# Roots of the norms by logarithm and exponential on ScalarE, merged key and query products, and the first norms on VectorE

## The chip, the cores and the metric

The kernel runs on one core of a Trainium2 chip. The metric is the device time in microseconds of one execution. A core has TensorE (PE; its weight loads are listed as PEld), VectorE (DVE), ScalarE (ACT), GpSimd (POOL) and SyncE (SP), which work through their own queues in order and wait for one another by semaphores; DMA queues move data beside them.

## The reference

A sequence of 8 x 512 tokens with 128 features, x of shape (8, 512, 128) in float32, goes through four residual layers, each on a normalised copy of x:

```python
x = x + _L0_attn_ref(_layernorm(x), ...)   # a gated linear scan over time
x = x + _L0_ffn_ref(_layernorm(x), ...)    # one 128x128 matrix, picked by argmax
x = x + _L1_attn_ref(_layernorm(x), ...)   # delta rule over time, 16 heads of 8
x = x + _L1_ffn_ref(_layernorm(x), ...)    # 8 experts, the best 2 for each token
```

`_layernorm` is `(x - mean) / sqrt(var + 1e-5)`. The first layer divides its two matrices W_in and W_out by their largest singular values, if these are over 1. Its scan has coefficients that are normalised per element. The third layer normalises a second time inside, makes query, key, value and a gate beta for every token, divides the key by its norm over the 8 features of a head, and runs, for every head,

```python
retrieval = S @ k_t
S = S + outer(beta_t * (v_t - retrieval), k_t)
o_t = S @ q_t
```

over the 512 steps. The fourth layer routes every token to two experts with 512 hidden units, gelu between the two products.

## The kernel before

**Tiling.** Tokens are taken in 32 tiles of 16 time steps x 8 sequences = 128 rows. Four tiles make a group (`g` from 0 to 7). For every group there is a first part (`first_layers`: `scanned`, `ssm_out`, `linear`), a preparation of the delta rule (`delta_in`), the delta rule itself (`delta_rule`), and routing (`route`). One or two groups together then go through the experts (`experts`): their rows are scattered by destination to DRAM with indirect DMAs of GpSimd, taken in blocks of 128 rows of one expert each, and gathered back.

**The delta rule.** It is sequential in time. A tile is done in four blocks of four steps, and inside a block the four steps are solved at once with a small triangular matrix (`tm`, the T matrix, the trace's `tmat`), which is made from the products of keys of a block at distance one, two and three and from beta. For each of the 128 blocks VectorE runs six instructions, each needing the one before: a product `so` of keys and queries with the state, a sum over it, the product with the T matrix (`prod`), a sum, the product with keys, and a sum that is the new state. Keys and queries in the layout for this come from `scratch` in DRAM into `kq`. Products of queries with keys inside a block go into `planes` (`qkp`) and then to the output matmuls.

**Norms.** `moments` takes sums of four tiles with VectorE's `bn_stats`. `factors` makes from them the factor 1/sqrt(var + eps) and the shift -mean times that factor, on GpSimd: a multiply-add (two if the second normalisation inside the delta layer is made at once, `norms == 2`), a power -0.5 against the constant `mhalf`, a product with the mean and a multiplication by -1. `normalised` applies factor and shift tile by tile on ScalarE. There are four norms for each group: of the input (`i`), after the first layer (`a`), before the delta rule (`b`, with both factors), and before the experts (`e`). The trace has them as `small_mvi`, `small_rstdi`, `small_shifti`, and with a, b and e.

**Products at a distance.** In `delta_in` six GpSimd instructions write `pd` (key with key one step apart, and three apart), `pc` (key with key and query with key, two apart) and `pb` (query with key, one and three apart); a seventh writes `pa` (the same step). TensorE then sums them over a head with `head_ones`.

**Singular values.** `spectral` squares each of the two matrices 24 times, with a division by the trace each third time; every squaring is a matmul, then a copy or scaling out of PSUM: VectorE's for the first matrix, ScalarE's for the second. `gain` comes from both.

**The order.** Instructions are not issued as they are written: a recorder (`Recorder`, `Plan`) keeps them with a number each, and `ORDER`, a list of all numbers, says in which sequence they go to the engines. Each engine takes its own in that sequence. A load of ScalarE's function table is put wherever the next function needs another set than the one loaded: logarithm and exponential are in one set (`LN_EXP`), tanh and gelu in another (`GELU_TANH`).

Of the kernel before, what the change touches and what calls it, by code (L numbers as in the profile page):

```python
# [9 lines left out]
F32 = mybir.dt.float32  # L10
# [3 lines left out]
ALU = mybir.AluOpType  # L14
# [344 lines left out]
def _cost(engine, name, n, kw):  # L359
# [28 lines left out]
    1, 7, 53, 56, 105, 50, 0, 13, 418, 54, 58, 115, 4, 17, 47, 55, 63, 41, 5, 6, 61, 9, 18, 40, 2, 3, 57, 8, 15, 60,  # L388
    422, 11, 14, 48, 74, 59, 16, 19, 108, 32, 10, 20, 45, 12, 23, 49, 46, 109, 44, 22, 338, 43, 67, 69, 110, 21, 354,
    70, 71, 111, 24, 30, 42, 324, 112, 25, 330, 26, 346, 113, 114, 27, 116, 124, 325, 126, 117, 72, 118, 339, 125,  # L390
    123, 326, 127, 327, 119, 131, 132, 128, 28, 129, 134, 130, 120, 328, 75, 121, 329, 122, 135, 65, 133, 388, 77,
    331, 138, 73, 386, 136, 139, 873, 347, 148, 137, 51, 387, 147, 66, 362, 390, 141, 355, 140, 341, 149, 153, 107,
    389, 142, 146, 391, 33, 150, 392, 83, 151, 85, 29, 154, 143, 84, 156, 454, 82, 393, 152, 37, 144, 145, 106, 88,
    157, 155, 35, 394, 89, 340, 158, 370, 322, 160, 80, 39, 76, 395, 31, 159, 161, 332, 170, 34, 163, 169, 333, 36,
    86, 171, 90, 162, 378, 175, 164, 334, 172, 78, 396, 62, 91, 178, 38, 165, 397, 68, 168, 173, 174, 166, 176, 167,
    335, 348, 179, 398, 177, 182, 336, 92, 180, 403, 399, 356, 181, 357, 183, 184, 402, 349, 192, 185, 191, 190, 401,
    193, 186, 342, 198, 194, 197, 358, 423, 195, 337, 400, 187, 359, 188, 189, 81, 405, 196, 200, 199, 52, 406, 93,
    202, 350, 201, 404, 407, 203, 204, 206, 205, 87, 207, 212, 351, 214, 213, 408, 208, 220, 215, 352, 209, 219, 210,
    343, 211, 409, 221, 222, 216, 217, 410, 224, 218, 223, 225, 94, 411, 95, 226, 229, 228, 96, 97, 227, 371, 230,
    98, 234, 236, 363, 235, 102, 231, 237, 99, 242, 104, 232, 241, 233, 412, 238, 100, 244, 239, 240, 243, 101, 245,  # L400
    246, 413, 248, 247, 249, 250, 258, 414, 251, 257, 456, 259, 256, 252, 263, 260, 264, 103, 455, 261, 262, 266,
    253, 458, 254, 459, 255, 267, 460, 265, 353, 415, 344, 270, 268, 457, 271, 269, 416, 461, 462, 272, 273, 279,
    417, 278, 274, 285, 286, 280, 420, 275, 276, 463, 288, 277, 281, 287, 282, 290, 419, 283, 464, 284, 424, 289,
    291, 421, 292, 425, 294, 293, 79, 379, 296, 295, 427, 297, 298, 465, 466, 299, 302, 303, 426, 307, 300, 345, 304,
    308, 301, 311, 309, 312, 428, 305, 429, 306, 310, 313, 430, 431, 314, 315, 316, 467, 317, 468, 318, 319, 320,
    360, 321, 469, 323, 471, 432, 474, 433, 472, 491, 592, 434, 373, 470, 364, 435, 436, 380, 473, 372, 365, 437,
    438, 475, 381, 439, 476, 440, 443, 441, 444, 442, 448, 445, 477, 446, 382, 447, 361, 490, 478, 449, 450, 479,
    451, 452, 480, 453, 522, 523, 525, 524, 481, 526, 593, 482, 527, 528, 529, 483, 530, 539, 531, 540, 532, 533,
    541, 64, 595, 542, 366, 594, 374, 367, 543, 536, 383, 544, 484, 375, 485, 545, 546, 486, 547, 537, 488, 596, 548,
    487, 549, 492, 554, 550, 376, 534, 552, 493, 551, 555, 553, 597, 563, 598, 599, 600, 556, 558, 560, 564, 601,  # L410
    561, 565, 557, 569, 559, 566, 660, 489, 570, 571, 574, 662, 575, 494, 602, 495, 576, 572, 661, 578, 573, 704,
    577, 603, 562, 579, 496, 497, 580, 498, 581, 499, 628, 567, 582, 500, 587, 568, 583, 1212, 502, 516, 606, 703,
    584, 588, 501, 585, 503, 663, 589, 608, 504, 586, 664, 368, 505, 590, 665, 506, 666, 510, 667, 668, 509, 669,
    508, 591, 670, 702, 607, 604, 671, 672, 535, 673, 629, 674, 605, 538, 675, 507, 676, 612, 610, 511, 677, 512,
    513, 678, 514, 679, 609, 680, 515, 681, 613, 377, 682, 517, 746, 689, 683, 690, 614, 744, 684, 691, 611, 685,
    518, 692, 686, 693, 745, 694, 705, 687, 695, 615, 519, 688, 706, 520, 696, 616, 707, 708, 617, 709, 697, 710,
    698, 618, 699, 711, 700, 521, 1143, 1142, 1213, 712, 1144, 619, 713, 1145, 384, 714, 1146, 715, 1214, 716, 620,
    717, 1147, 385, 718, 1148, 719, 621, 1152, 720, 721, 1149, 722, 1150, 1153, 1159, 723, 622, 1160, 724, 1151, 731,
    788, 725, 623, 732, 726, 1161, 1162, 786, 727, 733, 1215, 734, 728, 735, 787, 729, 736, 747, 1163, 737, 730, 748,
    624, 1164, 749, 1157, 750, 626, 751, 738, 752, 739, 1166, 740, 753, 741, 625, 1165, 742, 754, 1154, 755, 1167,  # L420
    627, 756, 743, 630, 1168, 757, 1172, 758, 1169, 759, 1170, 1174, 760, 1173, 1171, 761, 762, 1175, 763, 1178,
    1180, 764, 1176, 1183, 1181, 765, 1217, 1216, 1218, 1219, 1177, 1185, 701, 773, 766, 1194, 774, 1184, 767, 775,
    776, 768, 1179, 1220, 1182, 769, 1282, 777, 1280, 778, 770, 1189, 771, 789, 1221, 1281, 1186, 1156, 790, 779,
    1226, 772, 1190, 791, 792, 793, 780, 1191, 794, 1195, 1228, 631, 1227, 1196, 1192, 1198, 1222, 1193, 795, 1232,
    796, 1197, 781, 1233, 782, 828, 783, 1223, 633, 784, 797, 798, 799, 800, 632, 1199, 634, 801, 635, 1155, 636,
    1200, 637, 802, 1224, 803, 1201, 804, 805, 1234, 806, 785, 638, 1202, 1235, 807, 1203, 808, 1225, 1204, 815,
    1324, 640, 816, 1561, 1236, 1205, 817, 639, 818, 819, 809, 820, 641, 810, 642, 821, 811, 822, 812, 1207, 813,
    1323, 643, 1283, 1206, 1284, 814, 1208, 1285, 1322, 1286, 1237, 1287, 644, 1229, 1288, 823, 645, 824, 1289, 825,
    646, 649, 1230, 648, 826, 1290, 650, 647, 1291, 1292, 827, 1187, 651, 652, 829, 1231, 1293, 1188, 1294, 653,
    1238, 1295, 1209, 1296, 1297, 655, 1298, 1211, 1299, 1210, 654, 1300, 1239, 1249, 1301, 830, 1302, 831, 1240,  # L430
    656, 1366, 1303, 657, 658, 1304, 832, 1309, 1563, 1305, 833, 1310, 1241, 659, 1564, 1311, 1365, 1312, 1307, 1313,
    1492, 834, 1314, 1315, 1306, 1308, 835, 838, 1491, 837, 1316, 839, 1325, 836, 1493, 1494, 1562, 1317, 1326, 1495,
    1318, 1242, 1327, 1566, 1328, 1567, 1243, 840, 1329, 841, 1319, 1330, 1565, 1496, 1568, 1502, 1320, 1331, 1497,
# [209 lines left out]
def seq_kernel(  # L643
# [384 lines left out]
    def factors(mv, part, norms=1, bufs=2):  # L1028
# [4 lines left out]
        if norms == 2:  # L1033

            nc.gpsimd.tensor_scalar(rstd[:, 1], mv[:, :, 2], (1.0 + LN_EPS) / P, LN_EPS * LN_EPS, ALU.mult, ALU.add)
# [845 lines left out]
```

## Time and profile before

| what | value |
|---|---|
| median of 3 runs | 692.75 us (692.0 to 696.13) |
| the profiled execution | 694.65 us, span 693.0 us |
| granted TensorE clock, mean | 0.867 |
| busy: PE, VectorE, ScalarE, GpSimd | 514.9, 483.1, 465.4, 546.3 us |
| first and last `so` of the delta rule start at | 101.0 and 565.8 us |
| loads of ScalarE's table by the order's changes of set | 44 |

Times in the profile are microseconds from the start of the span. A group's line gives line, engine, operation, what it writes and reads, shapes and count, then busy time and the mean of one in ns, then the idle time of the engine ahead of it with what ended it. A line of waits gives who waited for whom, the total, how often, and the longest. A stage's line gives busy time and number of instructions of PE, PEld, VectorE, ScalarE, GpSimd, then the clock, the DMA share and GB/s. Nearly all instructions have the recorder's line L335, so they are told apart by the tiles they write.

### The profile page before, as it was taken

To read this page: it belongs to the slowest core of one execution; us is meant where nothing else is said; L and a number is where in the kernel's file an instruction comes from. 1 tells how busy PE (TensorE), PEld (TensorE's weight loads), DVE (VectorE), ACT (ScalarE), POOL (GpSimd) and SP (SyncE) were. 2 spreads that over 40 slices of the span, in tenths; PEclk is the share of its full clock that TensorE was granted. 3 is DMA by queue.
4 is the path that set the end of the run, shared out by engine and by line. 5 is a ranking of instruction groups with operands and counts; after the bars stand their busy time and mean duration, and the time that the engine had idled before them with its cause. 6 is when DMAs were issued, how large, how long until landed. Compare 5 with 4: busy or idle time off the path is not lost. (4 is left out here: it accounts for less than half of the span.)

```text
span 693.0 us, 10892 instructions
## 1 busy us (share of the span) xinstructions
PE 514.9 (74%) x2948; PEld 399.2 (58%) x2948; DVE 483.1 (70%) x1276; ACT 465.4 (67%) x1087; POOL 546.3 (79%) x682
## 2 busy tenths in 40 slices
PE   4886576876769777963768878877889769979970
PEld 3663224544348445652636766666668758978860
DVE  4565169999997899995899999878999970300111
ACT  2876757768775697883785988843986445846640
POOL 5566776699899979998869999987898886786634
PEclk9976586789788987997988999997999898999995
DMA  4991062352184636445346765555799855789852
GB/s 116 288 282 43 0 168 61 101 116 73 37 225 129 170 93 151 109 122 157 113 124 155 180 166 145 161 155 146 190 238 257 217 159 159 219 233 261 252 161 76
DMA packets 94977, 107.48 MB, mean 155 GB/s; under 512 B 8667, under 2 KB 68006, under 8 KB 94918
## 3 DMA queue, kind: packets, MB, share of 16 engines
q1 hardware_dynamic: 89616, 97.97, 52.1%
q0 software_dynamic: 4160, 8.53, 4.6%
q8 instruction: 25, 0.41, 0.3%
q10 hardware_dynamic: 1142, 0.29, 0.2%
q14 instruction: 34, 0.28, 0.1%
HBM read 84.93 MB, written 27.61 MB: 162 GB/s over the span
## 5 line engine op out<-in xcount | busy, mean ns | idle before, releaser
L335 ACT ACTIVATE hid<-ph,w1b 128x128 f32<-128x128 f32 x396 | 117.4, 376 | 53.6 <-PE ph L335 31.3
L335 PE MATMUL ph<-xbT,w1b 128*128 128x128 f32 x792 | 127.9, 292 | 13.3 <-DMA w1b<-w1b_dram 8.0
L335 PEld LDWEIGHTS ph<-xbT,w1b 128*128 128x128 f32 x792 | 112.1, 205 | 25.0 <-issue 11.2
L1595 PE MATMUL po<-w_sb,hid 128*128 x704 | 114.4, 288 | 5.2 <-DVE small_place L335 1.4
L1595 PEld LDWEIGHTS po<-w_sb,hid 128*128 128x128 f32 x704 | 99.1, 201 | 15.7 <-issue 7.5
L335 DVE TENSOR_TENSOR so<-kq,st 128x512 f32<-128x512 f32 x128 | 87.9, 687 | 13.1 <-POOL small_mine L335 7.8
L335 POOL DMA_INDIRECT back<-results,small_dest x64 | 61.9, 968 | 32.9 <-DMA results<-yb 16.2
L1533 POOL DMA_INDIRECT places<-xne,small_dest x64 | 63.6, 993 | 17.9 <-issue 13.5
L335 PEld LDWEIGHTS po<-wo,so 128*128 128x128 f32 x264 | 45.5, 239 | 36.4 <-issue 17.7
L335 DVE TENSOR_REDUCE st<-so 128x32 f32<-128x320 f32 x128 | 63.1, 493 | 4.8
L335 DVE TENSOR_REDUCE st<-st 128x64 f32<-128x320 f32 x128 | 63.6, 497 | 4.0
L335 PE MATMUL po<-wo,so 128*128 128x128 f32 x264 | 51.8, 333 | 19.1 <-DVE x L335 7.9
L335 PE MATMUL in<-b,head_ones 128*128 128x512 f32 x80 | 48.8, 695 | 14.4 <-POOL b L335 6.2
L335 DVE TENSOR_TENSOR st<-kq,st 128x256 f32<-128x256 f32 x128 | 54.6, 426 | 3.9
L304 ACT ACT_TABLE_LOAD x44 | 56.5, 1283 | 0.8
L335 PE MATMUL in<-f,wT 128*128 128x512 f32 x64 | 41.8, 750 | 10.8 <-DVE x L335 4.4
L335 PE MATMUL in<-b,wqkvb 128*128 128x512 f32 x64 | 40.6, 729 | 10.8 <-ACT b L335 3.8
L335 POOL TENSOR_TENSOR qkp<-qkp,upd 128x512 f32<-128x512 f32 x32 | 37.8, 1182 | 10.0 <-ACT upd L335 9.8
L335 DVE SCALAR_TENSOR_TENSOR fin<-back,small_weight,fin 128x128 f32<-128x128 f32 x16 | 5.1, 349 | 57.4 <-DMA back<-results,small_dest 50.1
L335 DVE TENSOR_TENSOR prod<-tmat,st 128x128 f32<-128x128 f32 x128 | 36.5, 285 | 10.3 <-POOL tmat L335 6.9
L335 DVE TENSOR_REDUCE st<-prod 128x32 f32<-128x128 f32 x128 | 37.5, 293 | 7.4 <-ACT upd L335 2.3
L335 POOL TENSOR_TENSOR so<-so 128x512 f32<-128x512 f32 x24 | 30.7, 1280 | 12.1 <-DVE so L335 10.7
(290 smaller groups left out, 1267.6 us busy)
## 6 DMA issues: line engine op xcount, KB each, us to landing
kq<-scratch SPq DMA_DIRECT2D x64, 512.0 KB
w1b<-w1b_dram SPq DMA_DIRECT2D x99, 258.0 KB
xb<-places SPq DMA_DIRECT2D x21, 256.0 KB
results<-yb SPq DMA_DIRECT2D x21, 256.0 KB
places<-yb SPq DMA_DIRECT2D x2, 1472.0 KB
w1b_dram<-in_L_ffn_w_dram SPq DMA_DIRECT2D x1, 2048.0 KB
scratch<-qn SPq DMA_DIRECT2D x8, 256.0 KB
scratch<-kn SPq DMA_DIRECT2D x8, 256.0 KB
```

Source lines behind the costliest of these rows:

```text
L304: self.hw.scalar.preload_act_table_set(switch)
L335: return method(*(on(x) for x in args), **{k: on(x) for k, x in kw.items()})
L1533: rows_out = hw.gpsimd.indirect_dma_start(out=table[0 : nblk * P, :], out_offset=bass.IndirectOffsetOnAxis(ap=at, axis=0), in_=src, in_off ...
L1595: return hw.tensor.matmul(out_.on(nc.banks), lhsT=src, rhs=w2_f[:, bass.ds(at + c * P, P)], start=(c == 0), stop=(c == NHB - 1),)
```

## The change

The power, its constant and the two multiply-adds of `factors` go; ScalarE takes the logarithm of the variance plus eps and the exponential of -0.5 times that, and VectorE makes the shift in one instruction. For group 0 (`leads`) `normalised` runs on VectorE. Key and query of a group lie in one tile (`knq`), and the products with a key one step apart, three apart and two apart are each made for key and query by one GpSimd instruction. The second matrix of `spectral` is copied and scaled by VectorE. The recorded instructions go from 4905 to 4850 (one fewer in each of 32 calls of `factors`, three fewer in each of 8 groups, one constant less, two more), and `ORDER` is a new list.

```diff
 ORDER = (
...
 )
...
-    WIDE = {"both": 2 * N, "xne": P, "w1b": NHB * P + NHB, "drive": N + B, "z": N + B, "kq": NR * QN, "prod": B * BL * BL}
+    WIDE = {"both": 2 * N, "xne": P, "w1b": NHB * P + NHB, "drive": N + B, "z": N + B, "kq": NR * QN, "knq": 2 * N, "dots": 2 * N, "prod": B * BL * BL}
...
-    mhalf = ctile([P, 2, NT], "mhalf")
-    nc.vector.memset(mhalf, -0.5)
...
+        ("eps_col", LN_EPS),
+        ("eps2_col", LN_EPS * LN_EPS),
...
-        nc.gpsimd.tensor_scalar(rstd[:, 0], mv[:, :, 2], 1.0 / P, LN_EPS, ALU.mult, ALU.add)
+        shift = stile([P, norms, NT], "shift" + part, F32, bufs)[:, :, 0:n]
+        spread = mv[:, :, 2]
+        nc.scalar.activation(rstd[:, 0], spread, AF.Ln, bias=eps_col, scale=1.0 / P)
         if norms == 2:
-
-            nc.gpsimd.tensor_scalar(rstd[:, 1], mv[:, :, 2], (1.0 + LN_EPS) / P, LN_EPS * LN_EPS, ALU.mult, ALU.add)
-        nc.gpsimd.tensor_tensor(rstd, rstd, mhalf[:, 0:norms, 0:n], ALU.pow)
-        shift = stile([P, norms, NT], "shift" + part, F32, bufs)[:, :, 0:n]
-        nc.gpsimd.tensor_mul(shift, mv[:, :, 1].unsqueeze(1).to_broadcast([P, norms, n]), rstd)
-        nc.gpsimd.tensor_scalar_mul(shift, shift, -1.0)
+            nc.scalar.activation(rstd[:, 1], spread, AF.Ln, bias=eps2_col, scale=(1.0 + LN_EPS) / P)
+        nc.scalar.activation(rstd, rstd, AF.Exp, scale=-0.5)
+        mean = mv[:, :, 1].unsqueeze(1).to_broadcast([P, norms, n])
+        nc.vector.scalar_tensor_tensor(shift, mean, -1.0, rstd, ALU.mult, ALU.mult)
         return rstd, shift
...
-    def normalised(src, rstd, shift, xn, norm=0):
+    def normalised(src, rstd, shift, xn, norm=0, leads=False):
         for i in range(src.shape[1]):
+            if leads:
+                nc.vector.tensor_scalar(
+                    xn[i], src[:, i, :], rstd[:, norm, i : i + 1], shift[:, norm, i : i + 1], ALU.mult, ALU.add
+                )
+                continue
...
-        nc.scalar.copy(xT, transposed(normalised(x, rstd, shift, tiles_of(xn.rearrange("p (i d) -> p i d", d=D)))))
+        nc.scalar.copy(xT, transposed(normalised(x, rstd, shift, tiles_of(xn.rearrange("p (i d) -> p i d", d=D)), leads=g == 0)))
...
-        nc.scalar.copy(xT, transposed(normalised(x1, rstd, shift, tiles_of(ptile([P, n, D], "f", FIRST)))))
+        nc.scalar.copy(xT, transposed(normalised(x1, rstd, shift, tiles_of(ptile([P, n, D], "f", FIRST)), leads=leads)))
...
-        xh = normalised(x2, rstd, shift, tiles_of(ptile([P, NT, D], "b3")), 1)
+        xh = normalised(x2, rstd, shift, tiles_of(ptile([P, NT, D], "b3")), 1, g == 0)
...
-        normalised(x2, rstd, shift, tiles_of(base))
+        normalised(x2, rstd, shift, tiles_of(base), 0, g == 0)
...
-        kn = ptile([P, N], "kn")
+        kq = ptile([P, 2, N], "knq")
+        kn, qn = kq[:, 0], kq[:, 1]
...
-        qn = ptile([P, N], "qn")
...
-        kb, qb, bb = by_block(kn), by_block(qn), by_block(beta)
-        pa, pb, pc, pd = (ptile([P, N], t) for t in ("b3", "b4", "b2", "b5"))
+        pairs = kq.rearrange("p x (k t) -> p x k t", t=BL)
+        kb, bb = pairs[:, 0], by_block(beta)
+        pa, pc = ptile([P, N], "b3"), by_block(ptile([P, N], "b2"))
+        dots = ptile([P, 2, N], "dots")
+        pd, pb = by_block(dots[:, 0]), by_block(dots[:, 1])
+        both = lambda v: v.unsqueeze(1).to_broadcast([P, 2] + list(v.shape[1:]))
+        apart = dots.rearrange("p x (k t) -> p x k t", t=BL)
         nc.gpsimd.tensor_mul(pa, qn, kn)
-        pb, pc, pd = by_block(pb), by_block(pc), by_block(pd)
-        nc.gpsimd.tensor_mul(pd[:, :, 0:3], kb[:, :, 1:4], kb[:, :, 0:3])
-        nc.gpsimd.tensor_mul(pd[:, :, 3:4], kb[:, :, 3:4], kb[:, :, 0:1])
-        nc.gpsimd.tensor_mul(pc[:, :, 2:4], kb[:, :, 2:4], kb[:, :, 0:2])
-        nc.gpsimd.tensor_mul(pc[:, :, 0:2], qb[:, :, 2:4], kb[:, :, 0:2])
-        nc.gpsimd.tensor_mul(pb[:, :, 0:3], qb[:, :, 1:4], kb[:, :, 0:3])
-        nc.gpsimd.tensor_mul(pb[:, :, 3:4], qb[:, :, 3:4], kb[:, :, 0:1])
+        nc.gpsimd.tensor_mul(apart[:, :, :, 0:3], pairs[:, :, :, 1:4], both(kb[:, :, 0:3]))
+        nc.gpsimd.tensor_mul(apart[:, :, :, 3:4], pairs[:, :, :, 3:4], both(kb[:, :, 0:1]))
+        nc.gpsimd.tensor_mul(
+            pc.rearrange("p k (x t) -> p x k t", x=2), pairs[:, :, :, 2:4], both(kb[:, :, 0:2])
+        )
...
-        nc.scalar.copy(a2, ps[:, :, 2:4])
-        nc.scalar.copy(by_block(planes[:, 1, :])[:, :, 2:4], ps[:, :, 0:2])
+        nc.scalar.copy(a2, ps[:, :, 0:2])
+        nc.scalar.copy(by_block(planes[:, 1, :])[:, :, 2:4], ps[:, :, 2:4])
...
-        spectral(0, nc.vector.tensor_copy, vector_scaled), spectral(1, nc.scalar.copy, nc.scalar.mul)
+        spectral(0, nc.vector.tensor_copy, vector_scaled), spectral(1, nc.vector.tensor_copy, vector_scaled)
...
-        x2 = linear(ssm_out(x, r))
+        x2 = linear(ssm_out(x, r), g == 0)
```

## The prediction

> **What bounds the kernel now.** I read the engine totals first, then the run in three stages (until the first distance product of the delta rule, from there to its last one, and the rest), then VectorE's waits in the middle stage, then the timeline of the first norms.
>
> ```profile
> PE 514.9 (74%) x2948; PEld 399.2 (58%) x2948; DVE 483.1 (70%) x1276; ACT 465.4 (67%) x1087; POOL 546.3 (79%) x682
> ```
>
> The stages (length, then busy time of PE, weight loads, VectorE, ScalarE, GpSimd):
>
> ```profile
> 0.00:101.00 101.00, 67.62 (x230) 41.24 (x231) 50.11 (x174) 64.73 (x149) 66.07 (x100) 0.79 0.54 149
> 101.00:566.50 465.50, 354.83 (x1988) 270.29 (x1986) 414.77 (x1034) 338.53 (x743) 401.57 (x503) 0.88 0.56 148
> 566.50:693.00 126.50, 92.42 (x731) 87.70 (x731) 18.17 (x70) 62.08 (x196) 78.62 (x81) 0.89 0.65 187
> ```
>
> GpSimd is busiest over the whole, but no stage is simply its own. In the first, no engine reaches 68%: a chain of dependent steps sets the time. In the second VectorE holds the chain of 128 blocks (`so` to `st`), and what keeps it waiting is this (engine, what it waited for, us in total, times, longest):
>
> ```profile
> DVE so L335 <- POOL small_mine L335: 7.8, 1, 7.8
> DVE prod L335 <- POOL tmat L335: 6.9, 4, 3.6
> DVE st L335 <- ACT upd L335: 2.3, 3, 1.6
> DVE small_runf L335 <- PE po L335: 2.2, 1, 2.2
> DVE x L335 <- ACT hid L335: 2.2, 1, 2.2
> ```
>
> All waits of that list come to 24.0 us; 15 of them name GpSimd. Without any wait the stage would last 465.5 - 24.0 = 441.5 us, so GpSimd's relief can give no more than that there. The third stage is TensorE's (92.4 of 126.5 us), with the last gather at its end.
>
> The norms of the first stage (start, duration, engine, what). GpSimd makes factors from the moments, then ScalarE applies them:
>
> ```profile
> 62.48 0.20 POOL L335 TENSOR_SCALAR small_rstda<-small_mva 128x4 f32<-128x4 f32 x1
> 62.77 1.02 POOL L335 TENSOR_TENSOR small_rstda<-small_rstda,mhalf 128x4 f32<-128x4 f32 x1
> 63.87 0.20 POOL L335 TENSOR_TENSOR small_shifta<-small_mva,small_rstda 128x4 f32<-128x4 f32 x1
> 64.15 0.23 POOL L335 TENSOR_SCALAR small_shifta<-small_shifta 128x4 f32<-128x4 f32 x1
> ```
>
> ```profile
> 65.30 1.64 ACT L335 ACTIVATE f<-x,small_shifta,small_rstda 128x128 f32<-128x128 f32 x4
> ```
>
> Nothing overlaps this for group 0, since all that follows needs it.
>
> **What the skill says.** "ScalarE: Activation LUTs", section "What ACT_TABLE_LOAD costs": a load takes 1283 ns for every set; the trace agrees:
>
> ```profile
> L304 ACT ACT_TABLE_LOAD x44 | 56.5, 1283 | 0.8
> ```
>
> Its section "Table sets: the hidden batching unit" puts ln and exp in one set and gelu in another, so a pair ln, exp costs one load at most, and one more to come back to gelu. "SBUF — State Buffer", section "Who interferes with whom": a VectorE instruction with two SBUF inputs and a GpSimd instruction that reads SBUF lock each other out. The trace agrees: the subtraction of 128x8 values `sc<-sc,ex` took 1.82 us, ending as GpSimd's 2.35 us sum ended. So less GpSimd work also shortens some VectorE work; I give that no number.
>
> **The change part by part.**
>
> *Factors.* 32 calls (8 groups, four norms). Mean GpSimd times per call: input 0.20+1.03+0.20+0.23 = 1.65; a 0.20+1.05+0.20+0.23 = 1.68; b 2x0.19+1.67+0.21+0.24 = 2.51; e 0.20+1.04+0.32+0.34 = 1.90 us. Times 8: 61.8 us leave GpSimd, some 41 of them in the middle stage (6 a, 7 b, 7 e there by the new order). ScalarE gets 2 instructions per call (3 for b) at 0.20 us: the 128x8 exponentials here took 0.19 to 0.21, a 128x32 one 0.22, so nothing hides in that bound. VectorE gets one of 0.20 us (between 0.14 for a 128x1 and 0.29 for a 128x8 operation).
>
> *Table loads.* Following the two order lists through and counting each change of set: 44 before, as in the trace, and 56 after: by stage 6, 36, 2 and 5, 47, 4. Middle stage of ScalarE: 11 x 1.28 = 14.1, plus 6 x 0.4 + 7 x 0.6 + 7 x 0.4 = 9.4, from 338.5 to 362 us: 79% of a stage of 456 us. Not the bound, if nobody waits for it in order.
>
> *The new wait.* The shift product sits in VectorE's queue and waits for ScalarE's exponential; 20 of them stand between blocks of the delta rule, where earlier VectorE made the moments and went on. In most, 2 to 12 us of other VectorE work stand between moments and shift; in three, under 1.8 us. Behind it wait the next block, then copies and output products. Charge: 20 x 0.23 = 4.6 us of work, and 4 us of waiting (lower end 0, upper end in the third rival).
>
> *Products of a distance.* Six GpSimd products of a group took 0.83+0.43+0.61+0.84+1.15+0.69 = 4.55 us. Three remain, of 768, 256 and 512 elements. These rows run at 2.15 to 3 ns an element:
>
> ```profile
> L335 POOL TENSOR_TENSOR b<-qn,kn 128x384 f32<-128x384 f32 x8 | 9.2, 1146 | 0.0
> L335 POOL TENSOR_TENSOR b<-kn 128x384 f32<-128x384 f32 x8 | 6.6, 827 | 0.3
> ```
>
> So 3.4 to 4.7 us; I take 3.9: 0.65 us a group, 5 us of GpSimd in all. But the first result, which the T matrix needs, comes after 1.9+0.73 instead of 0.83+0.43 us, and now needs the query too: +1.4 us on group 0's path.
>
> *First norms on VectorE, and the second matrix's copies.* 16 normalisations (0.48 us on ScalarE) and 26 copies or scalings (7.7 us in the order's sum) move to VectorE at about 0.29 us (the 128x128 copies there): 12 us more on VectorE in a stage where it idles 51 us; that idle time hides it.
>
> *Path of the first stage.* (1) Until `x1` at 60.0 us: both the 24 squarings and the first scan have to be done. The scan's ScalarE part runs from 21 to 48 us and shares ScalarE with the second matrix; about 16 of its operations there are 5 us. TensorE, in order, waits for those copies too. I take 4 us off (1 to 7). (2) Norm a: moments end at 61.54, factors 64.38, normalised at 66.94: 5.4 us; after: three instructions of 0.2, three hops of 0.06 and 4 x 0.29 = 2.0: -3.4. (3) Norm b: 71.86 to 76.46, 4.6 us; after 2.2: -2.4. (4) Products +1.4. (5) By the order two T matrix steps (1.13+0.37 us) come after the first `so`: -1.5. Sum -9.9: the first `so` at 91 us. The loads of `kq`, issued from 91.1 us on, come 8 us earlier with the key and the query; SP's queue has nothing new ahead of them.
>
> *Middle stage.* 441.5 + 4.6 + 0.8 (two T steps in, one 0.68 us sum out) = 446.9. Remaining waits: of the 24 us, 15 name GpSimd, and another 6 (`x`, `small_runf`, one `upd`) come, followed back, from a GpSimd step late in its queue. GpSimd's work falls from 401.6 by about 46, some 11%. I leave 6 of these waits and add the 4: 456.9, 8.6 less.
>
> *Last stage.* The new list leaves TensorE 164 and 168 expert products where there were 163 and 165; two more loads on ScalarE (2.6 us), mostly beside TensorE's queue; one factor call shorter by 1 us: +1.
>
> Sum: -9.9 - 8.6 + 1 = -17.5. The profiled execution took 694.65 us (span 693.0); it gives 677. The median shown, 692.75, gives **675 us**.
>
> **The rivals.**
> (A) Forecast, 675. For it: almost all of VectorE's waits end in GpSimd, which loses a ninth of its work, and the first norms stand bare on the path.
> (B) The wait moves: GpSimd's bursts stay (64 scatters of 0.99 us in rows of up to 16), so `so` and `tmat` wait as long, 21 us again, plus 4 at the shifts; the middle stage stays at 441.5+5.4+25 = 472, +6; the first gives 10, the last takes 1: 690. A version with half of that gives 683.
> (C) Slower: ScalarE becomes the bound through the in-order shift waits. All else as forecast without its 4 us of waiting gives 21.5; 20 shifts eat that from 1.1 us each on. If a load (1.28) and a gelu row behind it (4 x 0.38 less overlap, about 1.2) stand ahead of each, 2.5 us, it is 50 - 21.5 = 28 slower: 721; at half the shifts 696. Against: by the order most shifts have more VectorE work before them.
> (D) Everything goes: no waits left (446.9) and the first path shorter by 13: -13 - 18.6 + 1: 662.
>
> **Numbers.** Chances: A (668 to 682) 0.50, B (683 to 692) 0.20, C (693 to 721) 0.14, D (656 to 667) 0.16. A measurement tells about 1% (7 us) from no change. Faster by over 1% (below 685.8): A, D and half of B, 0.76. Within 1%: the other half of B and C's mild end, 0.15. Slower: 0.09. The range 660 to 693 leaves out C and the lowest third of D, 0.19 together.
>
> **What would show it.** The first `so` near 91 us; the stage from there to the last near 457; GpSimd about 66 us less busy; 56 loads; `prod<-POOL tmat` and `so<-POOL` waits below 10 us together; shift products with under 5 us of wait. Wrong if VectorE's wait list is led by ScalarE's `small_rstd`, or the first `so` stays near 100.

## The result, and the profile after

| what | before | after |
|---|---|---|
| median of 15 runs | 694.57 us (690.39 to 699.78) | 689.6 us (684.52 to 691.87) |
| ratio, 95% interval | | 0.9917 (0.9887 to 0.9946) |
| profiled execution, its span | 694.65, 693.0 us | 689.16, 687.4 us |
| granted TensorE clock, mean | 0.867 | 0.868 |
| `x` of group 0 after the first layer (x1) | 60.0 us | 65.3 us |
| first and last `so` | 101.0, 565.8 us | 99.5, 561.6 us |

The change gains 5 us, where 17.5 were forecast. Ratios here are always to the kernel before, run beside on the same chip; on three chips, those of e1 to e4, e13 to e16, and e17 and e18, it took 720 us instead of 694, and what these can and can't tell is said with their runs.

The engine totals and one group of the profile after:

```profile
PE 513.5 (75%) x2948; PEld 402.5 (59%) x2948; DVE 504.4 (73%) x1351; ACT 480.3 (70%) x1129; POOL 484.3 (70%) x522
...
L304 ACT ACT_TABLE_LOAD x56 | 71.8, 1283 | 1.0
```

GpSimd lost 62.0 us of work, ScalarE has 12 table loads more: the change does what it says. VectorE has 21.3 us more. The three stages of the kernel after, cut at the same events as before (columns as there):

```profile
0.00:99.50 99.50, 66.44 (x228) 44.07 (x228) 68.02 (x225) 57.05 (x131) 50.39 (x60) 0.79 0.54 150
99.50:562.30 462.80, 356.19 (x1982) 272.94 (x1983) 417.23 (x1054) 357.98 (x797) 360.18 (x387) 0.87 0.55 147
562.30:687.40 125.10, 90.88 (x741) 85.53 (x739) 19.16 (x75) 65.30 (x202) 73.75 (x76) 0.91 0.68 197
```

Against 101.0, 465.5 and 126.5 us, the stages are 1.5, 2.7 and 1.4 us shorter; -9.9, -8.6 and +1 had been forecast. VectorE's waits in the middle stage, after:

```profile
DVE x L335 <- PE in L335: 9.5, 5, 2.7
DVE x L335 <- PE po L335: 2.9, 1, 2.9
DVE st L335 <- ACT upd L335: 2.4, 1, 2.4
DVE so L335 <- PE po L335: 2.0, 2, 1.2
DVE small_shifte L335 <- ACT small_rstde L335: 0.6, 1, 0.6
...
DVE so L335 <- POOL tmat L335: 0.2, 1, 0.2
```

GpSimd has almost gone from the list by name, and the new shift waits cost 0.6 us. Yet the waits still sum to 19.1 us (24.0 before). They now name TensorE, so the names alone don't tell what was late; the experiments had to. The first norms of group 0, in the timeline of the kernel after:

```profile
68.15 0.28 ACT L335 ACTIVATE small_rstda<-small_mva,eps_col 128x4 f32<-128x4 f32 x1
68.70 0.66 DVE L335 SCALAR_TENSOR_TENSOR small_shifta<-small_mva,small_rstda 128x4 f32<-128x4 f32 x1 [1.22 <-ACT small_rstda L335]
69.40 3.23 DVE L335 TENSOR_SCALAR f<-x,small_rstda,small_shifta 128x128 f32<-128x128 f32 x4
69.69 2.34 POOL L335 TENSOR_TENSOR both<-both,f 128x1024 f32<-128x1024 f32 x1 [0.35 <-ACT both L335]
...
78.32 0.17 DVE L335 SCALAR_TENSOR_TENSOR small_shiftb<-small_mvb,small_rstdb 128x8 f32<-128x8 f32 x1 [0.80 <-ACT small_rstdb L335]
78.53 1.12 DVE L335 TENSOR_SCALAR b<-x,small_rstdb,small_shiftb 128x128 f32<-128x128 f32 x4
```

The same four normalisations take 1.12 us in norm b and 3.23 us in norm a, where GpSimd's 2.34 us sum starts beside them.

### The profile page after: what moved, and what is told of

Same layout as the page of the kernel before. It is cut to its first block, busy times and chain, and to the rows that moved or that the text cites. A ratio compares the mean times of both kernels' runs of the same rounds, so it can differ in the third digit from the quotient of the medians.

```text
span 687.4 us, 10830 instructions
## 1 busy us (share of the span) xinstructions
PE 513.5 (75%) x2948; PEld 402.5 (59%) x2948; DVE 504.4 (73%) x1351; ACT 480.3 (70%) x1129; POOL 484.3 (70%) x522
## 5 line engine op out<-in xcount | busy, mean ns | idle before, releaser
L335 PE MATMUL ph<-xbT,w1b 128*128 128x128 f32 x792 | 124.5, 287 | 18.5 <-DMA w1b<-w1b_dram 12.7
L335 PEld LDWEIGHTS ph<-xbT,w1b 128*128 128x128 f32 x792 | 108.0, 199 | 31.9 <-issue 17.9
L1601 PE MATMUL po<-w_sb,hid 128*128 x608 | 98.4, 284 | 5.2 <-ACT hid L335 4.2
L1601 PEld LDWEIGHTS po<-w_sb,hid 128*128 128x128 f32 x608 | 85.0, 198 | 14.5 <-ACT hid L335 8.0
L335 PE MATMUL po<-wo,so 128*128 128x128 f32 x248 | 49.7, 331 | 20.9 <-DVE so L335 10.1
L335 PEld LDWEIGHTS po<-wo,so 128*128 128x128 f32 x248 | 43.3, 239 | 31.1 <-DVE so L335 12.5
L335 DVE SCALAR_TENSOR_TENSOR fin<-back,small_weight,fin 128x128 f32<-128x128 f32 x16 | 5.0, 351 | 56.7 <-DMA w1b<-w1b_dram 44.1
L335 POOL TENSOR_TENSOR f<-f,f 128x512 f32<-128x512 f32 x24 | 30.4, 1273 | 19.9 <-ACT f L335 19.9
```

The source lines that it names most:

```text
L335: return method(*(on(x) for x in args), **{k: on(x) for k, x in kw.items()})
L1601: return hw.tensor.matmul(out_.on(nc.banks), lhsT=src, rhs=w2_f[:, bass.ds(at + c * P, P)], start=(c == 0), stop=(c == NHB - 1),)
```

## The experiments

### The order that GpSimd really gets (middle stage)

The account of the kernel before says that each engine takes its own instructions in the order of the list. For GpSimd the trace shows otherwise. Its timeline in the kernel after, about 455 us:

```profile
455.08 1.08 POOL L1539 DMA_INDIRECT places<-xne,small_dest  x1 [0.58 <-DVE small_dest L335]
...
470.48 0.97 POOL L1539 DMA_INDIRECT places<-xne,small_dest  x1 [0.31 <-issue]
471.46 1.27 POOL L335 TENSOR_TENSOR so<-so 128x512 f32<-128x512 f32 x1
```

The first two lines are the ends of a row of 13 scatters, one about every 1.28 us. The list has the sum `so<-so` after the seventh. The code tells why. `emit` fixes the order of PE, VectorE, ScalarE and SP, but ties GpSimd's instructions only pairwise, each to the one before it (`keep_in_program_order`). `scatter` declares every scatter independent of the earlier ones of its table, since "every row has places of its own", and that also takes away the tie between a scatter and a scatter right before it. Such a scatter is tied to nothing earlier, and is issued ahead of what the list puts between. In the list of the changed kernel the longest rows of scatters are 8 and 7; built, 13 and 11. In the kernel before they are 4 in the list, and 9 and 7 built.

What waits for the late sums is TensorE, which multiplies them by the output matrix (total, times, longest, after):

```profile
PE in L335 <- POOL so L335: 11.4, 1, 11.4
PE po L335 <- POOL so L335: 7.4, 5, 5.1
```

The 11.4 us end at 330.0 us, behind a row of scatters from 313 us on. The 5.1 us end at 472.8 us, as the sum of 471.46 us is done, and VectorE's `x<-in`, whose product stands behind in TensorE's queue, waits 2.7 us until 474.3 us. So waits that name TensorE lead back to GpSimd.

**Held to the list.** The edit (e1, e6 on the changed kernel, e2, e9 on the kernel before) ties each of GpSimd's transfers to the last instruction before it that is no transfer, and each such instruction to the transfers just before it:

```diff
     def emit(self):
...
+        order_only = mybir.DependencyInfo(mybir.DependencyClass.NoSync, mybir.DependencyReason.DATA)
+        last, run = [], []
...
                 if op.engine == "gpsimd":
                     self.tc.keep_in_program_order(made)
+                    moved = "dma" in type(made.ins).__name__.lower()
+                    for name in last if moved else run:
+                        self.tc.add_manual_dep(made.ins, name, order_only, reason="the list's place")
+                    last, run = (last, run + [made.ins.name]) if moved else ([made.ins.name], [])
```

Changed kernel, held:

> The changed kernel with GpSimd's program held to the written list: a scatter that follows a scatter keeps its place behind the operation that stands before both in the list (in the built program such scatters had lost that place, so that 13 of them stood in a row where the list puts an addition of the recurrence after the seventh). Nothing is computed differently. Theory 1 (the 19.4 us of VectorE's waits left in the middle stage come from the scatters' bursts on GpSimd): the waits at 325, 332 and 474 us go, the middle stage falls from 462.8 to 454 to 458, the time to 681 to 685. Rival (the waits belong to TensorE's and ScalarE's own queues, as the waits name them): within 1.5 us of the changed kernel's 689.6.

Kernel before, held:

> The kernel before with GpSimd's program held to its written list in the same way. Theory 1: here too the bursts cost something, 4 to 10 us, 685 to 691. Rival: within 1.5 us of 694.6.

Measured on one chip: e1 732.48 us, 1.0166 (1.013 to 1.0201); e2 709.81 us, 0.9856 (0.9819 to 0.9894). So it helped the kernel before, while the changed one, held, was slower than the kernel before. But this is a chip where the kernel before took 720.65 us, the changed kernel itself did not run on it, and e1's last stage there was 162 us long, where the kernel after has 125; what the edit does can't be read from that total. The pair was taken again, with the changed kernel itself beside it:

> The changed kernel itself, unaltered, as the measure for the kernels run beside it: in e1 to e4 the kernel before took 720.7 us and not 694.6, so those need it too. If the chip is like the first one: 0.9917 of the kernel before. If it is like that of e1 to e4, theory: 743 to 748 us, for e3 and e4, which are the changed kernel with small alterations, took 743.6 and 749.1 there; the rival says 715, and then e3's one move cost 28 us.

> The kernel of e1 (the changed kernel with the scatters held to the written list), beside the unaltered changed kernel. Theory 1 (bursts of scatters hold the recurrence): 5 to 13 us below e5, the middle stage shorter by as much, the waits named at 325, 332 and 474 us gone. Rival: within 1.5 us of e5.

> The kernel of e2 again (the kernel before with the scatters held to its written list). Theory 1 (the bursts of scatters hold up both kernels): the wait of 7.8 us at 330 us and its like go, the middle stage falls from 464.8 us to 453 to 458, the time to 0.980 to 0.990 of the kernel before; then a part of what the change was to bring could be had without it. Rival (the kernel before has GpSimd so full, 402 of 465 us, that the order on it matters less than its load): 0.995 or more.

| run | us | ratio to before | first `so` | middle stage | VectorE's waits in it |
|---|---|---|---|---|---|
| e5, changed | 689.78 | 0.9931 (0.9904 to 0.9959) | 98.4 | 462.4 | 18.2 |
| e6, changed, held | 677.22 | 0.9752 (0.9719 to 0.9785) | 98.6 | 449.6 | 4.7 |
| e9, before, held | 684.42 | 0.9864 (0.9843 to 0.9886) | 101.1 | 458.9 | 12.4 |

The same place in e6's timeline: the sum now comes after seven scatters, 18 us earlier, and six more scatters follow it.

```profile
452.17 0.97 POOL L1545 DMA_INDIRECT places<-xne,small_dest  x1 [0.31 <-issue]
453.25 1.26 POOL L341 TENSOR_TENSOR so<-so 128x512 f32<-128x512 f32 x1
454.68 0.98 POOL L1545 DMA_INDIRECT places<-xne,small_dest  x1 [0.16 <-issue]
```

And e6's middle stage, with what is left of VectorE's waits:

```profile
98.60:548.20 449.60, 348.45 (x1985) 267.57 (x1985) 418.10 (x1054) 358.17 (x798) 359.55 (x386) 0.90 0.58 151
```

```profile
DVE x L341 <- PE po L341: 1.1, 1, 1.1
DVE x L341 <- PE in L341: 1.1, 3, 0.5
...
```

The work of VectorE, ScalarE and GpSimd is within 1 us of the kernel after; TensorE's is lower at a higher clock. The stage is 13 us shorter, and 14 us of waits are gone; TensorE's waits for `so` in it fall from the 18.8 us above to 5.6. The waits of VectorE were TensorE's in name, but the edit moves GpSimd's instructions alone: what had made TensorE late was work of GpSimd behind a row of scatters. The granted clock is no rival for this: it rose in e6's stage (0.90, 0.88 in e5), but e9's stage is 6.6 us shorter than that of the kernel before at the same 0.88. With both lists held, the change brings 684.4 to 677.2 us; 10 us in the kernel before and 12.6 us in the changed one are lost to the same cause.

**The roots in the new list.** In e4 (not held) and e10 (held) the old body of `factors` stands in the changed kernel, its GpSimd instructions at the places of the new ones:

```diff
-        nc.scalar.activation(rstd[:, 0], spread, AF.Ln, bias=eps_col, scale=1.0 / P)
+        nc.gpsimd.tensor_scalar(rstd[:, 0], mv[:, :, 2], 1.0 / P, LN_EPS, ALU.mult, ALU.add)
...
-        nc.scalar.activation(rstd, rstd, AF.Exp, scale=-0.5)
...
-        nc.vector.scalar_tensor_tensor(shift, mean, -1.0, rstd, ALU.mult, ALU.mult)
+        nc.gpsimd.tensor_tensor(rstd, rstd, mhalf[:, 0:norms, 0:n], ALU.pow)
...
+        nc.gpsimd.tensor_mul(shift, mv[:, :, 1].unsqueeze(1).to_broadcast([P, norms, n]), rstd)
+        nc.gpsimd.tensor_scalar_mul(shift, shift, -1.0)
```

> The changed kernel with one part undone: the norms' roots are taken by GpSimd's power again, in the list's places of the logarithm and the exponential; 8 table loads fewer, some 66 us more of GpSimd. Theory 1 (the roots are the part that brought the gain in the middle stage): VectorE's waits for GpSimd's T matrices come back, the middle stage goes from 462.8 to 468 or more, the time to 694 or more. Rival (the gain is the new list's or the merged products'): within 2 us of 689.6.

> The kernel of e6 (changed, scatters held to the list) with the norms' roots by GpSimd's power again, in the places of the logarithm and the exponential; 48 table loads and not 56, some 66 us more of GpSimd. Theory 2 (with the scatters in their places the roots bring what the prediction gave them, 8 to 10 us of the middle stage): 0.985 to 0.990 of the kernel before, where e6 had 0.9752, with waits for GpSimd's T matrices back. Rival (the list alone brings it): 0.978 or less.

e4 took 749.07 us, 1.0395 (1.0361 to 1.0429), on the first chip; the changed kernel itself did not run there. e10 took 699.19 us, 1.0063 (1.0041 to 1.0085): 22 us more than e6. Its first `so` came 5.2 us later, its middle stage lasted 464.7 us (e6: 449.6), and VectorE waited 24.5 us in it (4.7):

```profile
DVE x L341 <- PE in L341: 8.1, 5, 4.1
DVE prod L341 <- POOL tmat L341: 6.8, 3, 4.9
...
```

So when GpSimd's 40 us come back to the middle stage, VectorE waits 20 us more and the stage is 15 us longer. This list was made for roots on ScalarE, so a part of that may be the places of the instructions and not their load. The other comparison, each kernel held to the list made for it, is e6 against e9: the middle stage goes from 458.9 to 449.6 us and VectorE's waits from 12.4 to 4.7. That is 9.3 us, roots and merged products together, where the forecast had 8.6. The forecast's mechanism holds where the list is kept.

In the first stage, too, the roots show. From x1 to the first `so` e10 takes 40.3 us and e6 34.2: from the end of the moments to the last normalised value norm a takes 7.6 us against 5.8, norm b 6.0 against 2.1. e4 against e1, on one chip, says the same (39.8 and 34.3 us). x1 itself comes earlier with the power: 62.7 us in e4, 65.4 in e1 (63.5 in e10, 64.4 in e6).

### The first stage up to x1

**The bank.** Group 0's scan input in the changed kernel, and what VectorE does with it:

```profile
54.97 0.69 DVE L335 TENSOR_TENSOR drive<-f,in 128x512 f32<-128x512 f32 x1 [1.69 <-PE in L335]
56.12 1.24 DVE L335 TENSOR_TENSOR_SCAN z<-decay,drive 128x520 f32<-128x520 f32 x1 [0.46 <-DVE drive L335]
```

`drive` waits for a product of TensorE that, by the code, has nothing to do with it. The list has the scan input's matmul (number 416) one place ahead of the ScalarE instruction that frees a PSUM bank (394; TensorE's products go to banks of PSUM and are read from there). Both banks of its kind are held there, so it takes one that soon counts as free: squarings and then a projection of group 1 write the same bank, and `drive` has to wait for that one, and is formed from it. (So, by the code, a part of the computation is changed in the kernel after, and in e1, e3 to e7 and e10: group 0's scan input is taken from another product. The work done is the same.) e11 has the two exchanged, beside the held list:

```diff
 ORDER = (
...
-    38, 216, 220, 416, 394, 395,
+    38, 216, 220, 394, 416, 395,
...
```

> The kernel of e6 with one matrix product moved by two places in the list. In the changed list this product, one factor of the scan's input of group 0, takes its PSUM bank while both banks are held; later products take the same bank, the last of them group 1's projection, so that group 0's scan input waits for that one and is formed from it. Moved behind the operation that gives a bank free, it has one of its own, and group 0's scan input is what it should be. Theory 3 (this wait made x1 of group 0 late): the wait of 1.4 to 1.7 us before the scan's input goes, x1 comes at 62.5 to 63 us, the time falls by 1 to 2 us against e6. Rival (the trace sums hold x1 anyway): within 1 us of e6, 0.974 to 0.976.

It took 672.51 us, 0.9692 (0.9669 to 0.9714), the fastest of all, 22 us under the kernel before. Its drive waits for nothing:

```profile
52.40 0.67 DVE L341 TENSOR_TENSOR drive<-f,in 128x512 f32<-128x512 f32 x1
...
61.70 0.75 DVE L341 SCALAR_TENSOR_TENSOR x<-in,gain,x 128x512 f32<-128x512 f32 x1
```

x1 comes at 61.7 instead of 64.4 us (e6), the first `so` at 95.6 instead of 98.6, and VectorE waits 2.2 us in the middle stage of 447.1 us. So the 5 us of the kernel after are not bought by its wrong product: with the right one the kernel is faster still (e11 against e6). That leaves x1 1.7 us later than in the kernel before, where the forecast has it 4 us earlier.

**Group 0's chain earlier.** e12: as e11, but the loads of `x` first in SP's and ScalarE's queues and the chain from them to the scan 27 places earlier in the list.

> The kernel of e11 with group 0's chain 27 places earlier in the list from its second statistics to its scan, and its loads of x ahead of other loads on both queues (in the changed kernel the last of them are issued at 9.6 to 12.2 us, in the kernel before by 7.2). Theory 3 (the list's place of group 0's chain, not ScalarE's load, made x1 late): x1 at 59 to 61 us and not 65.3, the first product of the recurrence with a T matrix 3 to 5 us earlier, the time 3 to 5 us below e6: 0.968 to 0.971. Rival (the T matrices come late through ScalarE and GpSimd between x1 and the recurrence): x1 earlier, the time within 1.5 us of e6.

678.7 us, 0.9751 (0.9724 to 0.9777): 6 us more than e11. `drive` came at 49.8 us, 2.6 us earlier, but:

```profile
51.46 2.29 DVE L341 TENSOR_TENSOR_SCAN z<-decay,drive 128x520 f32<-128x520 f32 x1 [0.74 <-POOL decay L341]
...
56.45 0.27 DVE L341 COPY xne<-po 128x128 f32<-128x128 f32 x1
```

The last copy of the squarings stands behind the scan in VectorE's queue and ended at 56.7 us; in e11 it started at 52.2. x1 came at 65.7 us. The theory that the late loads of `x` (issued until 13.8 us in the changed kernel, until 8.4 before) set x1 fell: with both chains on VectorE, what one gains the other loses.

**The end of the squarings earlier.** From the end of the last copy of the squarings to `gain` it takes 11.5 us in the kernel after (53.3 to 64.8 us) and 6.4 in the kernel before (53.1 to 59.5). e3 and e7 put the traces of the two squared matrices, from which `gain` is made, ahead of group 0's scan in the changed list; e18 does so in e11's:

```diff
 ORDER = (
...
-    417, 418, 456, 308, 309, 313, 310,
+    456, 308, 309, 313, 417, 310, 418,
...
```

(The two lines show the sequence of the operations concerned alone, in e7; others stand between them. 417 and 418 are `drive` and the scan, 308 to 313 belong to the traces, 456 is a projection of group 1.)

> The changed kernel with one thing moved in the written list: on VectorE the trace sums of the two squared matrices stand ahead of the multiplication that makes the scan's input and of the scan of group 0, and GpSimd's steps for the gain ahead of its product with the scan; the two waits (1.69 and 0.46 us) and two operations (0.69 and 1.24 us) no longer stand before the gain. Theory 1 (the first stage's gain was lost in VectorE's queue behind the squarings): x1 of group 0 comes at 61.5 to 62.5 us and not at 65.3, the time falls by 2.5 to 3.5 us, to 686 to 687. Rival (group 0's scan, late because of its norms, holds x1 just as well): x1 within 1 us of 65.3, the time within 1 us of 689.6.

> The kernel of e3 (the trace sums ahead of the scan's input and the scan on VectorE), beside the unaltered changed kernel. Theory 1: x1 of group 0 about 3.5 us earlier, the time 2 to 3.5 us below e5. Rival (the scan, late for its norms, holds x1 as well): within 1 us of e5.

> The kernel of e11 with the trace sums ahead on VectorE: the scan's input is formed in the time in which they wait for TensorE, the scan comes behind them, and GpSimd's product with the scan stays ahead of the gain. Theory (x1 of group 0 is held by the gain, 0.4 us ahead of it in e11, and the gain by the two operations of the scan in front of the trace sums): x1 0.5 to 1.5 us earlier than in e17, the time 0.5 to 1.5 us less. Rival (both ways end together): x1 within 0.5 us of e17, no difference.

e3 took 743.59 us, 1.0322 (1.0277 to 1.0368), on the first chip. e7 took 688.33 us, 0.9907 (0.9883 to 0.9932), within 1.5 us of e5 beside it. `gain` came at 61.1 us, earlier by about 3 us, and then x1 waited for the other branch, the scan's product:

```profile
65.06 0.75 DVE L335 SCALAR_TENSOR_TENSOR x<-in,gain,x 128x512 f32<-128x512 f32 x1 [3.48 <-PE in L335]
```

e18 (724.75 us; e17, e11's kernel beside it, 721.79) had x1 at 63.5 against 61.9 us and the first `so` 2.9 us later. So no order of the two chains tried here in the new list gave x1 before 61.7 us.

### The parts alone

e8 and e13 do one part in the kernel before, in its own list; e14, e15 and e16 take one part back in e11's kernel. e13 to e18 ran on chips where the kernel before took 720 us. There e17, which is e11's kernel, is within 1 us of e11 up to 405 us and loses after it, so they are read up to the first `so` and by totals among themselves. How far x1 and the first `so` vary by themselves can be seen in the kernel after and e5, one kernel: 65.3 and 64.3 us, 99.5 and 98.4. The stretch between the two is steadier: it was 34.2 to 34.3 us in the kernel after, e1, e5 and e6, and 33.9 and 34.2 in e11 and e17.

```diff
-        spectral(0, nc.vector.tensor_copy, vector_scaled), spectral(1, nc.scalar.copy, nc.scalar.mul)
+        spectral(0, nc.vector.tensor_copy, vector_scaled), spectral(1, nc.vector.tensor_copy, vector_scaled)
```

That is e13 (the second matrix of `spectral` on VectorE, old list); e15 is the reverse in the new one.

> The kernel before with one part of the change alone: the second matrix's squarings copied and scaled on VectorE too, in the same places of its written list. The prediction's step (1): x1 of group 0 comes 4 us earlier than 60.0 (1 to 7), the time 0.992 to 0.996 of the kernel before. Rival (the 24 squarings are a chain through TensorE, their end doesn't depend on which engine copies, and VectorE then has both): x1 at 60 to 62 us, 0.999 to 1.004.

> The kernel of e11 with the second matrix's squarings copied and scaled by ScalarE again. The prediction's step (1): x1 of group 0 later than 61.7 us by 4, the time 0.974 to 0.976 of the kernel before. Rival (VectorE, with both chains, group 0's norms and the scan before the trace sums, is what holds x1): x1 at 59.5 to 61.5 us, the time within 1.5 us of e11 or below, 0.966 to 0.970.

e13: 719.17 us, 0.9982 (0.9965 to 0.9998); x1 at 59.7 us, where the runs of the old list with ScalarE's copies have 60.0 to 60.4: 0.7 us at most. e15: 727.91 us, 1.0099 (1.0065 to 1.0134); x1 at 65.7 against e17's 61.9, the first `so` 3.8 us later, the total 6 us more. A relief of the size of step (1), 4 us, is there in the new list only, which is made for it.

```diff
-    def normalised(src, rstd, shift, xn, norm=0):
+    def normalised(src, rstd, shift, xn, norm=0, leads=False):
         for i in range(src.shape[1]):
+            if leads:
+                nc.vector.tensor_scalar(
+                    xn[i], src[:, i, :], rstd[:, norm, i : i + 1], shift[:, norm, i : i + 1], ALU.mult, ALU.add
+                )
+                continue
```

That is e8 (group 0's norms on VectorE, factors still by GpSimd's power, old list, with `leads` handed on as in the change); e14 passes `False` for `leads` in e11's kernel.

> The kernel before with one part of the change alone: group 0's four norms (in, a and the two b) computed on VectorE, in the same places of its written list; roots by power and the products as before. The prediction's view: norm a and norm b of group 0 get shorter, 2 to 4 us below the kernel before. Rival, after the trace of the changed kernel: VectorE's norm of the input stands between the squarings and its norm a beside a GpSimd operation takes 2.4 us more, so that nothing is won: within 1 us of the kernel before, or slower.

> The kernel of e11 (changed, scatters held, own bank) with group 0's norms (in, a, b) on ScalarE again. The prediction (norm a and norm b shorter by 3.4 and 2.4 us on VectorE): slower than e11 by 2 to 5 us, 0.972 to 0.976 of the kernel before. Rival, after e8: within 1.5 us of e11 (0.967 to 0.971), or faster, since VectorE is then free for the squarings.

e8: 697.32 us, 1.0031 (1.0018 to 1.0045). Norm a was done at 65.5 us instead of 66.9, but x after the second layer came at 70.3 us, 70.4 before: the gain is lost again right behind it. e14: 721.19 us, 1.001 (0.999 to 1.003), its first `so` at 98.0 against 96.1 us in e17; the total is the same within the spread. 0.8 us of this are there at x1 already (62.7 against 61.9), no more than x1 varies by itself; from x1 on it takes 35.3 us against 34.2. So the norms on VectorE are worth about 1 us there in the new list, nothing in the old one. And the gain is norm b's: from the end of the moments to the last normalised value norm b takes 3.5 us in e14 and 2.1 in e17, but norm a 4.3 us on ScalarE and 5.8 on VectorE.

e16 makes the six products of a distance one by one again in e11's kernel, with the merged tiles kept:

```diff
-        nc.gpsimd.tensor_mul(apart[:, :, :, 0:3], pairs[:, :, :, 1:4], both(kb[:, :, 0:3]))
+        nc.gpsimd.tensor_mul(pd[:, :, 0:3], kb[:, :, 1:4], kb[:, :, 0:3])
+        nc.gpsimd.tensor_mul(pb[:, :, 0:3], qb[:, :, 1:4], kb[:, :, 0:3])
...
```

> The kernel of e11 with the merged key and query products taken apart again, each merged operation giving two in its place (six operations on the same tiles instead of three). The prediction (the merged form puts 1.4 us on the path to the first T matrix and nothing elsewhere): 1 to 2 us earlier first product of the recurrence, or at most the same time as e11. Rival (fewer, larger operations save GpSimd's fixed time in each group): slower than e11 by 1 to 4 us.

720.74 us, 1.0002 (0.9981 to 1.0023); the first `so` at 97.1 us, 1.0 us later than e17. But x1, which stands ahead of all these products, came 1.2 us later too (63.1 us), and from x1 on it takes 34.0 us against 34.2. So merging them neither cost nor gained group 0 anything that these runs can tell.

### One kernel on two chips

> The kernel of e11 again. If the kernel before takes 694 us here: 0.969 again, 671 to 674 us. If it takes 720 us, e14 to e16 can be read against it: the prediction of e15 (ScalarE's share of the squarings back: 3 us slower) gives 723 to 725 for this kernel, that of e14 (norms on VectorE worth 2 us) 719.

The same kernel took 672.51 us as e11 and 721.79 us as e17 (1.0011, 0.9987 to 1.0035). Their middle and last stages, e11 first:

```profile
95.60:542.70 447.10, 348.11 (x1985) 265.63 (x1985) 418.12 (x1054) 358.46 (x798) 359.92 (x387) 0.91 0.57 153
542.70:670.60 127.90, 92.42 (x736) 87.84 (x736) 19.31 (x74) 65.05 (x202) 73.64 (x75) 0.89 0.67 192
```

```profile
96.10:557.70 461.60, 355.80 (x1981) 271.81 (x1982) 418.10 (x1053) 357.76 (x793) 361.53 (x389) 0.88 0.55 147
557.70:718.40 160.70, 100.31 (x743) 94.53 (x741) 18.36 (x75) 66.93 (x206) 72.40 (x74) 0.81 0.55 154
```

Up to the 89th block of the delta rule the two are equal within 1 us: its `so` starts at 404.7 and 405.3 us. Then e17 loses 15 us in the middle stage and some 32 in the last (the cut shown stands 0.7 us ahead of the stage's end). TensorE's longest waits in its last stage:

```profile
PE ph L341 <- issue: 20.8, 3, 11.3
...
```

In "issue" the engine waits for nothing that the profile shows, here for up to 11.3 us at once. What it waited for, and why this kernel takes 49 us more on such a chip and the kernel before 26, stays open. The 5 us of the result are not touched by it: the kernel before and the changed one both ran without it, and e5 repeats them. But the gains told here hold for chips where the kernel before takes 694 us. Where it takes 720, none of the eight runs with the new list was faster than it (ratios 1.0002 to 1.0395); the old list, held (e2, 0.9856), was.

## Why the prediction was wrong in size

The direction was right, and much of the accounting: GpSimd's 62 us (66 said), 56 loads, a middle stage without waits of 444 us in the kernel after (462.8 - 19.1; 446.9 said), ScalarE's 358.0 us in it (362 said), the shifts' waits at 0.6 us, so rival C did not come about. The miss is 11.9 us against the profiled execution: 8.4 in the first stage, 5.9 in the middle one, less 2.4 in the last.

| step | forecast | measured |
|---|---|---|
| (1) until x1 | -4 | +5.3 |
| (2) norm a | -3.4 | +0.4 |
| (3) norm b | -2.4 | -2.5 |
| (4) products, (5) T steps, and the rest to the first `so` | -0.1 | -4.7 |
| middle stage | -8.6 | -2.7 |
| last stage | +1 | -1.4 |

**Middle stage: "I leave 6 of these waits and add the 4".** This is the step that failed there. It took the row of waits that name GpSimd to shrink with GpSimd's work. 19.1 us stayed, in other names. B's reason, "GpSimd's bursts stay", is what e6 shows, with rows of 13 and 11: with the scatters in the places that the list gives them, 4.7 us of waits remain and the time is 677.2. That the time came out where rival B had it (690) is luck all the same: B had 10 us off the first stage and 6 more in the middle one, and it was 1.5 off the first and 2.7 off the middle one; and the longest row of scatters in the trace of before is 9, not 16. That e6's 677.2 is close to the 675 forecast is partly chance too, since its first stage is 7.5 us longer than forecast and the middle stage 7.3 us shorter. What the forecast lacked was the difference between the list and what is built, which the trace of before already held: it shows 9 scatters in a row where the list has 4.

**Step (1), "I take 4 us off (1 to 7)".** This is the larger miss. It came out 9.3 us worse: the squarings ended no earlier (53.3 us, 53.1 before), and from there to `gain` it took 5.1 us more. 2.7 of the 9.3 are the bank (x1 in e11 against e6). The reason given, that ScalarE is relieved, is true and worth 3.8 us in the new list (e15), but the cost was put at nothing: "that idle time hides it". VectorE's work in the first stage rose by 17.9 us, not 12, and in e12 the copies and the scan took each other's place on it: the idle time was there in sum, not at the time when it was needed. With its bank in order and ScalarE relieved, e11 still has x1 at 61.7 us, 1.7 later than the old list without either, so the new list gives up some 5.5 us (1.7 and the 3.8) elsewhere before x1. How these divide is not settled. The sharing of VectorE is one part; the roots are another, which the forecast did not count ahead of x1: with the power put back x1 came 2.7 us earlier on one chip (e4 against e1) and 0.9 in e10 against e6; the traces, ended 5 us later after the last copy, are a third that e7 and e18 could move but not turn into time. TensorE's granted clock from 40 to 60 us was 0.62 (0.76 before), which no run varied by itself; x1 did not follow it in e6 (0.50, 64.4 us) and e11 (0.59, 61.7 us).

**Step (2), norm a.** The 2.0 us forecast became 5.8 (66.8 to 72.6 us). The logarithm started 1.3 us after the moments, behind other work in ScalarE's queue; the shift product took 0.66 us instead of 0.2, ending with a GpSimd product that had started before it; and one of the four normalisations stood still during GpSimd's sum, which accounts for 2.1 of the 3.23 us. The Trainium skill has the rule: "SBUF — State Buffer", section "Who interferes with whom", names `tensor_scalar` among the VectorE operations that can, under conditions, take the ports they share with GpSimd, and says that the engine which comes later then stands fully until the other ends. The prediction cited the section for operations with two inputs only, and gave it no number. The trace agrees with it: 1.12 us for the four in norm b, 3.23 beside the 2.34 us sum. In e8, with no such sum beside it, norm a's four took 1.11 us. The move of norm a to VectorE, counted as a gain, was a loss of 1.5 us (e14 against e17).

**The rest to the first `so`.** From x1 on, 34.2 us against 41.0: -6.8, where steps (2) to (5) said -5.9. The sum held though norm a's part came to nothing. By the runs that take one part back, the roots are most of it (6.2 us in e10 against e6, 5.5 in e4 against e1) and the norms on VectorE about 1 (e14); the products, forecast at +1.4, are at nothing (e16). From the first `so` to the first `prod` it is 2.4 us (1.4 before), since two T steps moved behind: 1.0 less ahead of it, where 1.5 was forecast. Parts taken out one at a time need not add up to the whole, and here they come to somewhat more.

**The last stage** is 1.4 us shorter, with 125.1 us; e5, the same kernel, had 127.4 and e6 127.8, so this lies within what it varies by.

## What to carry to other kernels

Before a wait is credited to an engine's load, look at the order in which that engine got its work: a declared independence can take away an ordering with it, and rows of up to 13 transfers ahead of sums of 1.3 us cost 12.6 us here, more than the 5 that the whole change brought. Idle time of an engine hides moved work only where the idle stretch lies; if the moved work and the critical chain meet on the engine, one of the two pays. An operation that another engine's memory access can block is to be priced from both cases, 1.12 and 3.23 us here, and by what the other engine does at that moment.

## What the runs showed of the hardware that was not expected

- GpSimd's scatters of 128 rows come about 1.28 us apart in a row (0.97 us each and 0.30 between), with nothing that the profile shows to wait for.
- Four 128x128 normalisations on VectorE took 1.12 us alone and 3.23 us beside one GpSimd sum of 128x1024 values that lasted 2.34 us; on ScalarE, beside the same sum, they took 1.63 us (e14).
- An exponential of 128x4 values took 0.19 to 0.21 us on ScalarE without a bias column, a logarithm of as many 0.28 to 0.30 us with one.
- A scan of 128x520 values took 1.24 us with no GpSimd product beside it, and 2.29 us in e12, where a product of 1.27 us had begun 0.1 us before it.
- One kernel took 672.5 us on one chip and 721.8 us on another, within 1 us of each other until 405 us; the cause is open.
